# The lead-in of a state-space kernel: norm powers, taps from PSUM, moments, a row of b, W_D as a diagonal

## The chip, the cores and the metric

The kernel runs on one core of one Trainium2 chip. The metric is device time in microseconds (us) of one launch; the kernel before takes 1954.29 us, the median of three runs (1954.05 to 1954.67). Five engines work side by side, each on its own in-order queue, and wait for each other on semaphores: PE (TensorE, matrix products), DVE (VectorE), ACT (ScalarE), POOL (GpSimd) and SP (SyncE, which here only issues DMA transfers). SBUF is the working memory and PSUM holds the results of PE.

## The reference, cut to what matters

Input x is 4 sequences of 1024 rows of 256 numbers. Four layers follow each other: a selective state-space layer, a layer with routed experts and an MLP, a linear attention, and the second layer's kind once more. The change touches the first layer alone:

```python
rn = resid * rsqrt(mean(resid * resid, -1) + EPS) * norm_w   # resid = layernorm(x)
skip, x_in = rn @ skip_w.T, rn @ in_w.T
xp = pad(x_in, (K - 1, 0))
conv = conv_b + sum(xp[:, k:k + L, :] * conv_w[:, k] for k in range(K))   # K = 4 taps
x = silu(conv)
delta = softplus(x @ wd1.T @ wd2.T + wd2_b)
Bm, Cm = x @ wB.T, x @ wC.T
h = exp(delta * A) * h + (delta * x) * b          # a scan over the rows, N = 16 states
y = sum_n h * c + x * W_D
return resid + (y * silu(skip)) @ out_w.T
```

So each row is normalised twice: by a layernorm, then by its root mean square.

## The kernel before, in words

The 4096 rows are cut into 8 groups of G = 512; E = 512 channels make EC = 4 tiles of 128 partitions ("channels" 0 to 3 below). `ssm` runs the first layer with an order written out by hand: `Pinned` keeps every instruction in program order on its engine. The main loop (from L941) goes over `s` = group x state and two halves: DVE does two scans (`tensor_tensor_scan`, L966) and two weighted sums (`sum_up`, L918) per half; ACT makes the decays `a` (`decay`, L907), POOL the inputs `u` = dx x row of b (`times_b`, L888), PE transposes h. The rows of b come from DRAM: `row` (L880) has SP broadcast one row to 128 partitions into a tile `bt`, of which there are two. Beside the scan of one group, `prepare` readies the next, and `tick` chooses what else is put between.

The first group has nothing to hide beside, so `first_group` (L715) is its own piece, the lead-in, and it ends with the first scan:

- SP loads the x of group 0 in four pieces, in_wT, skip_wT and the x of group 1 (L184 to L190); ACT's queue issues the small weights and then out_wT and down_w (L191 to L201).
- PE transposes the identity 48 times into a bank that nobody reads (L720).
- `moments(0)` gives mean and variance on DVE. The two norms' factors s1 and s2 are made one after the other (L727 to L733): a power on POOL, three small DVE operations, a second power on POOL, one more DVE operation. Then DVE normalises (`rn`, L739), PE transposes, DVE and ACT take one half each to SBUF with norm_w (`rnT`).
- `w_in(c)` (L760) multiplies by in_wT, one PSUM bank per channel. `taken` (L767) has ACT copy the bank to `xin` in SBUF, behind three columns of zeros, and apply the last tap and conv_b into `xc`; DVE adds the other three taps from `xin`, shifted.
- Per channel, ACT's silu, then PE's products with wd1 (`dt1`) and wbcT (`bc`). `taken(2)` and `taken(3)` stand between the silus. After them come the moments and factors of group 1 (L793 to L797) and b1, s1 of group 0.
- DVE copies `dt1` and `bc` out; `bc` goes to DRAM; PE multiplies by wd2 (`z`), ACT makes `delta` (Softplus), DVE `dx`. The first row of b is a product with ones (`b0`, in PSUM), which DVE copies to a `bt` tile (L821).
- W_D x xc is made in place, channels 0 and 1 on POOL (L837), 2 and 3 on ACT (L860); PE transposes the result into `acc` in the steps q = 1 and q = 2 (L863).

SP's next loads are the second row of b (L933), the x of groups 2 and 3, and small router weights.

Of the kernel before, what the change touches and what calls it, by code (L numbers as in the profile page):

```python
# [12 lines left out]
F32 = mybir.dt.float32  # L13
AF = mybir.ActivationFunctionType
ALU = mybir.AluOpType
# [35 lines left out]
class Net:  # L51
# [89 lines left out]
    def ssm(self, xs, hs, behind):  # L141
# [6 lines left out]
        with ExitStack() as ctx:  # L148
# [39 lines left out]
            skip_w0 = spare[:, :KD, :]  # L188
            sp.dma_start(out=skip_w0, in_=io["skip_wT"].rearrange("(k p) m -> p k m", p=P))
            load_x(1)  # L190
# [9 lines left out]
            out_w = self.load_rows(late, "out_wT", EC, D)  # L200
            down_w = self.load_rows(late, "down_w", IC, D)  # L201
# [4 lines left out]
            def rsqrt(out, v):  # L206
                pool.tensor_scalar(out, v, EPS, None, ALU.add)
                pool.tensor_tensor(out, out, self.mhalf.to_broadcast(list(out.shape)), ALU.pow)
# [47 lines left out]
            def factors(g, less, var):  # L256
                s1 = late4.tile([P, TG], F32, tag="s1", name="s1")
                s2 = late4.tile([P, TG], F32, tag="s2", name="s2")
                rsqrt(s1, var)
                yield 0  # L260
                pool.tensor_tensor(s2, s1, s1, ALU.mult)
                pool.tensor_tensor(s2, s2, var, ALU.mult)
                rsqrt(s2, s2)
                yield 0
                pool.tensor_tensor(s2, s2, s1, ALU.mult)
# [13 lines left out]
            def bank(shape, name):  # L279
                return mm.tile(shape, F32, tag="mm", name=name)  # L280
# [434 lines left out]
            def first_group():  # L715
# [4 lines left out]
                for i in range(48):  # L720
                    pe.transpose(cold[:, :P], self.ident, self.ident)
                mhalf = self.mhalf.to_broadcast([P, TG])
# [3 lines left out]
                b1, b2 = (late2.tile([P, TG], F32, tag=f"{n}0", name=n) for n in ("b1", "b2"))  # L726
                dve.tensor_scalar(s1, var, EPS, None, ALU.add)  # L727
                pool.tensor_tensor(s1, s1, mhalf, ALU.pow)
                dve.tensor_tensor(s2, s1, s1, ALU.mult)
                dve.tensor_tensor(s2, s2, var, ALU.mult)  # L730
                dve.tensor_scalar(s2, s2, EPS, None, ALU.add)
                pool.tensor_tensor(s2, s2, mhalf, ALU.pow)
                dve.tensor_tensor(s2, s2, s1, ALU.mult)  # L733
# [16 lines left out]
                xin = one.tile([P, EC, KC - 1 + G], F32, tag="xe", name="xin")  # L750
                pool.memset(xin[:, :, : KC - 1], 0.0)
# [40 lines left out]
                act.copy(carry, xin[:, :, G:])  # L792
                mv = moments(1)  # L793
                less = late2.tile([P, TG], F32, tag="sum", name="less1")
                pool.tensor_scalar(less, mv[:, :, 0], -1.0, None, ALU.mult)
                for _ in factors(1, less, mv[:, :, 1]):
                    pass  # L797
                pool.tensor_tensor(b1, mean, s1, ALU.mult)
                pool.tensor_scalar(b1, b1, -1.0, None, ALU.mult)
                pool.tensor_scalar(s1, s1, 1.0, None, ALU.add)  # L800
# [9 lines left out]
                bts[0] = thr.tile([P, G], F32, tag="bt", name="bt")  # L810
                for c in range(EC):
                    ps = bank([P, G], "z")
                    mul(ps, [(wd2[:, c * P : (c + 1) * P], dt1)])
                    act.activation(delta[:, c, :], ps, AF.Softplus, bias=wd2_b[:, c : c + 1])
                    if c == 1:

                        b0 = hp.tile([P, G], F32, tag="hT", name="b0")
                        mul(b0, [(ones, bc[:1, :])])
                for c in range(EC):
                    if c == 2:  # L820
                        dve.tensor_copy(bts[0], b0)  # L821
                    dve.tensor_tensor(dx[:, c, :], delta[:, c, :], xc[:, c, :], ALU.mult)
# [31 lines left out]
                def start(q):  # L854

                    decay(2 * q + 2)
                    decay(2 * q + 3)
                    if q == 0:
                        evac(cT, ps[:, :, N:])
                        for c in (2, 3):  # L860
                            evac(xc[:, c, :], xc[:, c, :], scale=w_d_col[:, c : c + 1])
                        return
                    pair = [(t, begun(xc, t)) for t in (2 * q - 2, 2 * q - 1)]  # L863
                    for t, p in pair:
                        evac(acc[:, t, :], p)
# [67 lines left out]
            row(1)  # L933
            for g in range(2, 4):
                load_x(g)
# [894 lines left out]
```

## Time and profile before

| | us |
|---|---|
| median of 3 runs | 1954.29 |
| the profiled execution | 1952.51 |
| its span, first to last instruction | 1950.8 |
| DVE, PE, ACT, POOL busy | 1545.6, 1772.8, 1178.8, 924.2 |
| first `rn` / first tap / `dt1` copy / first scan start | 9.39 / 15.39 / 27.20 / 35.63 |
| fifth scan / ninth scan start | 42.21 / 49.88 |

The profile comes from one execution. A line of its timeline has the start in us from the span's start, the duration (of several merged instructions, xcount, from the first start to the last end), the engine, the source line, the operation with out<-in, and in brackets how long the engine had been idle and what released it. Nearly every line says L46, that of the helper that pins the order, so instructions are told apart by their tiles. "skip_w" is also the name shown for views into the same buffer (`spare`), such as `rnT`. A matmul of 32-bit numbers shows as two records. A line of the table by windows gives the bounds, then the length, then the busy time of PE, PEld (its weight loads), DVE, ACT and POOL, then PEclk, the clock granted to TensorE as a share of full speed.

The lead-in is the first 36 us of 1951. From there to about 1100 us DVE paces the layer: its busy time is 98.23 of the 100 us from 100 to 200, and 386.39 of the 400 us from 400 to 800.

### The profile page before, as it was taken

What the parts mean: (1) busy time and instruction counts of PE and PEld (TensorE: products, weight loads), DVE (VectorE), ACT (ScalarE), POOL (GpSimd) and SP (SyncE); (2) the same over time, 40 slices, a digit from 0 to 9 for tenths busy, and PEclk for the clock granted to TensorE, in tenths of its full rate; (3) what the DMA queues carried; (4) which work ended last, traced back from release to release, by engine and by line L of the source; (5) the groups of instructions that cost most, each with busy time, mean ns of one, the idle gap of its engine ahead of it and who ended that gap; (6) DMA issues with size and microseconds to landing.
All of it is one profiled execution on the core that took longest, in us unless ns stands there. A gap on an engine that the chain in (4) does not pass through costs nothing.

```text
span 1950.8 us, 22751 instructions
## 1 busy us (share of the span) xinstructions
PE 1772.8 (91%) x7450; PEld 1141.0 (58%) x7450; DVE 1545.6 (79%) x2637; ACT 1178.8 (60%) x2335; POOL 924.2 (47%) x746
## 2 busy tenths in 40 slices
PE   7777789989899898898878999899999999999999
PEld 4445446556456564564645756666666566655665
DVE  6999999999999999999999989834549655434551
ACT  5877788887987878877564663844434333323330
POOL 4978998899888998888861000121111000000000
PEclk9969799999999999999989999999999999999999
DMA  4111121221212212212123121110000000000000
GB/s 142 49 39 55 50 81 55 82 72 64 88 57 80 69 51 87 77 45 80 55 89 122 60 81 49 60 65 1 1 1 1 11 11 12 0 12 11 11 11 11
DMA packets 79927, 97.47 MB, mean 50 GB/s; under 512 B 7360, under 2 KB 53312, under 8 KB 79808
## 3 DMA queue, kind: packets, MB, share of 16 engines
q1 hardware_dynamic: 74592, 90.66, 14.9%
q10 hardware_dynamic: 5216, 5.36, 0.9%
q8 instruction: 59, 0.97, 0.2%
q14 instruction: 60, 0.49, 0.1%
HBM read 83.15 MB, written 12.85 MB: 49 GB/s over the span
## 4 chain that ended last, share of the span: by engine, by line
PE 34%; DVE 13%; ACT 5%; issue 1%; POOL 1%; DVEq 0%; ACTq 0%; POOLq 0%
PE ps L135 23%; PE o L46 2%; PE at L46 1%; PE up L46 1%; DVE eq L46 1%; DVE acc L46 1%; DVE eq L1397 1%; DVE code L1405 1%; PE st L1469 1%; DVE h L46 1%; DVE tb L46 1%; PE route L1303 1%; PE down L46 1%; ACT tb L46 1%; PE emb L46 1%
## 5 line engine op out<-in xcount | busy, mean ns | idle before, releaser
L46 POOL TENSOR_TENSOR u<-dx,bt 128x1024 f32<-128x1024 f32 x255 | 601.6, 2361 | 79.7 <-DVE h L46 69.7
L46 DVE TENSOR_TENSOR_SCAN h<-a,u 128x512 f32<-128x512 f32 x512 | 608.2, 1226 | 16.8 <-ACT a L46 14.4
L46 PE MATMUL hT<-ident,h 128*128 128x128 f32 x2048 | 310.5, 292 | 105.4 <-DVE acc L46 105.1
L46 ACT ACTIVATE a<-delta,a_neg 128x512 f32<-128x512 f32 x512 | 340.1, 689 | 96.5 <-DVE h L46 95.7
L46 PEld LDWEIGHTS hT<-ident,h 128*128 128x128 f32 x2048 | 245.4, 149 | 242.8 <-DVE acc L46 196.6
L46 DVE SCALAR_TENSOR_TENSOR acc<-hT,cT,acc 128x512 f32<-128x512 f32 x512 | 354.2, 731 | 13.5 <-PE hT L46 12.8
L1726 DVE TENSOR_TENSOR act<-s,ps 128x512 f32<-128x512 f32 x64 | 43.9, 686 | 146.3 <-PE ps L135 145.5
L46 PE MATMUL up<-hT,up_w 128*128 128x512 f32 x256 | 134.6, 652 | 10.1 <-ACT up_v L46 10.0
L1724 ACT ACTIVATE s<-ps 128x512 f32<-128x512 f32 x64 | 38.2, 597 | 162.7 <-PE ps L135 162.6
L46 PE MATMUL gate<-hT,gate_w 128*128 128x512 f32 x256 | 122.1, 600 | 0.0
L135 PE MATMUL ps<-hT,w_gate_w 128*128 128x512 f32 x256 | 120.6, 592 | 0.0
L135 PE MATMUL ps<-hT,w_up_w 128*128 128x512 f32 x256 | 120.5, 592 | 0.0
L135 PE MATMUL ps<-w_down_w,act 128*128 128x256 f32 x512 | 117.5, 381 | 3.0 <-DVE x L1500 3.0
L46 PE MATMUL down<-w_down_w,av 128*128 128x256 f32 x512 | 118.2, 379 | 0.0
L46 POOL TENSOR_TENSOR xc<-xc,tap 128x512 f32<-128x512 f32 x84 | 108.8, 1296 | 18.8 <-ACT tap L46 18.7
L135 PEld LDWEIGHTS ps<-w_down_w,act 128*128 128x128 f32 x512 | 95.7, 190 | 21.4 <-DVE x L1500 8.8
L46 ACT ACT_TABLE_LOAD x77 | 98.8, 1283 | 14.8 <-DMA w_wd2T<-in_wd2T 7.3
L46 PEld LDWEIGHTS down<-w_down_w,av 128*128 128x128 f32 x512 | 94.8, 190 | 17.0 <-issue 5.3
L1387 ACT ACTIVATE tb<-d,ex 128x64 f32<-128x64 f32 x256 | 62.0, 333 | 53.9 <-DVE ex L1377 53.9
L46 PEld LDWEIGHTS up<-hT,up_w 128*128 128x128 f32 x256 | 48.8, 206 | 60.6 <-issue 42.0
L46 PE MATMUL out<-w_out_wT,y 128*128 128x256 f32 x256 | 67.6, 411 | 18.3 <-DVE y L46 18.3
L135 PEld LDWEIGHTS ps<-hT,w_up_w 128*128 128x128 f32 x256 | 48.5, 190 | 57.7 <-issue 56.4
(299 smaller groups left out, 3032.4 us busy)
## 6 DMA issues: line engine op xcount, KB each, us to landing
bt<-bcd SPq DMA_DIRECT2D x127, 256.0 KB, 3.3
gate_w<-in_gate_w SPq DMA_DIRECT2D x64, 128.0 KB, 2.3
up_w<-in_up_w SPq DMA_DIRECT2D x64, 128.0 KB, 2.2
in_wT<-in_in_wT SPq DMA_DIRECT2D x8, 512.0 KB, 5.0
hs<-hT SPq DMA_DIRECT2D x8, 512.0 KB, 2.9
xs<-xw SPq DMA_DIRECT2D x8, 512.0 KB, 2.7
hT<-hs SPq DMA_DIRECT2D x8, 512.0 KB, 4.9
x<-xs SPq DMA_DIRECT2D x8, 512.0 KB, 4.2
```

The costliest lines, as they stand in the source:

```text
L46: return self.tc.keep_in_program_order(f(*args, **kw))
L135: self.nc.tensor.matmul(ps, lhsT=lhsT, rhs=rhs, start=i == 0, stop=i == len(pairs) - 1)
L1303: nc.tensor.matmul(ps[:, t, m, :], lhsT=h[:, k, col], rhs=w["scores"][t][:, k, :], start=k == 0, stop=k == KD - 1,)
L1387: nc.scalar.activation(tbv[:, m, i, :], d[:, M4 + m, 0:NKEY], AF.Copy, scale=ex[:, m, i : i + 1],)
L1397: dve.tensor_tensor(eq, v[:, M4:, :].unsqueeze(2).to_broadcast(shk), r[:, M4:, :].unsqueeze(3).to_broadcast(shk), ALU.is_gt,)
L1405: dve.tensor_reduce(code.rearrange("p m j -> p (m j)"), eq.rearrange("p m j b -> p (m j) b"), AX.X, ALU.add,)
L1469: self.nc.tensor.transpose(st[:, c, :], tb[:, i, c * P : (c + 1) * P], self.ident)
L1724: nc.scalar.activation(s, pg, AF.Silu)
L1726: nc.vector.tensor_tensor(a, s, pu, ALU.mult)
```

## The change

1. The two powers no longer follow each other: with var the variance, s2 = ((1+EPS) var + EPS²)^-½ is taken directly, and s1 = (var + EPS)^-½ beside it. In the first group the order is s2, then s1; in `factors` (all later groups) three small POOL operations fall away.
2. The taps read the PSUM bank instead of `xin`; the ACT copy to `xin` goes, and a copy of three columns to `carry`, once per channel, is put behind the taps. The first tap of channel 3 goes to ACT and POOL.
3. `taken(2)` and `taken(3)` both stand behind the first silu. The moments and factors of group 1 move up, ahead of the taps; on SP the x of group 1 moves ahead of skip_wT.
4. The first row of b comes through DRAM, like the others (`row(0)`); `b0` stays for the first two `u`. The product b0 moves behind the four z.
5. W_D x xc is a PE product with a diagonal matrix that POOL makes from the identity; it writes `acc`'s start in the steps q = 0 and q = 1.
6. out_wT and down_w are loaded by SP, behind the second row of b and ahead of the x of groups 2 and 3.
7. 40 idle transposes instead of 48.

```diff
@@ ssm: loads, factors
+            load_x(1)
             sp.dma_start(out=skip_w0, in_=io["skip_wT"].rearrange("(k p) m -> p k m", p=P))
-            load_x(1)
...
-            out_w = self.load_rows(late, "out_wT", EC, D)
-            down_w = self.load_rows(late, "down_w", IC, D)
...
+            def both_norms(eng, out, var):
+                eng.tensor_scalar(out, var, 1.0 + EPS, EPS * EPS, ALU.mult, ALU.add)
@@ first_group
-                for i in range(48):
+                for i in range(40):
                     pe.transpose(cold[:, :P], self.ident, self.ident)
...
+                both_norms(dve, s2, var)
+                rsqrt(s2)
                 dve.tensor_scalar(s1, var, EPS, None, ALU.add)
-                pool.tensor_tensor(s1, s1, mhalf, ALU.pow)
-                dve.tensor_tensor(s2, s1, s1, ALU.mult)
-                dve.tensor_tensor(s2, s2, var, ALU.mult)
-                dve.tensor_scalar(s2, s2, EPS, None, ALU.add)
-                pool.tensor_tensor(s2, s2, mhalf, ALU.pow)
-                dve.tensor_tensor(s2, s2, s1, ALU.mult)
+                rsqrt(s1)
...
+                w_d = spare[:, 2 * KD, :].rearrange("p (c e) -> p c e", c=EC)
+                for c in range(EC):
+                    pool.tensor_scalar(
+                        w_d[:, c, :], self.ident, w_d_col[:, c : c + 1], None, ALU.mult
+                    )
+                mv = moments(1)
...
                 def taken(c, ps):
-                    act.copy(xin[:, c, KC - 1 :], ps)
                     act.activation(
                         xc[:, c, :], ps, AF.Identity, scale=conv_w[:, c, KC - 1 :],
                         bias=conv_b[:, c : c + 1],
                     )
                     for k in range(KC - 1):
-                        dve.scalar_tensor_tensor(
-                            xc[:, c, :], xin[:, c, k : k + G], conv_w[:, c, k : k + 1],
-                            xc[:, c, :], ALU.mult, ALU.add,
-                        )
+                        late = KC - 1 - k
+                        to, part, by = xc[:, c, late:], ps[:, : G - late], conv_w[:, c, k : k + 1]
+                        if c == EC - 1 and k == 0:
+                            t = spare[:, 2 * KD + 1, : G - late]
+                            act.activation(t, part, AF.Copy, scale=by)
+                            pool.tensor_tensor(to, to, t, ALU.add)
+                        else:
+                            dve.scalar_tensor_tensor(to, part, by, to, ALU.mult, ALU.add)
+                    act.copy(carry[:, c, :], ps[:, G - KC + 1 :])
...
                     act.activation(xc[:, c, :], xc[:, c, :], AF.Silu)
-                    if c + 2 < EC:
-                        taken(c + 2, xins[c + 2])
                     if c == 0:
+                        taken(2, xins[2])
+                        taken(3, xins[3])
                         sums = bank([P, G], "dt1"), bank([2 * N, G], "bc")
...
-                bts[0] = thr.tile([P, G], F32, tag="bt", name="bt")
+                row(0)
...
-                for c in (0, 1):
-                    pool.tensor_scalar(
-                        xc[:, c, :], xc[:, c, :], w_d_col[:, c : c + 1], None, ALU.mult
-                    )
+                def by_w_d(t):
+                    ps = bank([P, E], "xdT")
+                    for c in range(EC):
+                        pe.matmul(
+                            ps[:, c * P : (c + 1) * P], lhsT=xc[:, c, t * P : (t + 1) * P],
+                            rhs=w_d[:, c, :], start=True, stop=True,
+                        )
+                    return ps
@@ after first_group
             row(1)
+            out_w = self.load_rows(late, "out_wT", EC, D, sp)
+            down_w = self.load_rows(late, "down_w", IC, D, sp)
```

More of the change, by code (lines that the diff above doesn't have):

```diff
@@ L204, in ssm, with rsqrt @@
             carry = wp.tile([P, EC, KC - 1], F32, tag="carry", name="carry")
-            def rsqrt(out, v):
-                pool.tensor_scalar(out, v, EPS, None, ALU.add)
-                pool.tensor_tensor(out, out, self.mhalf.to_broadcast(list(out.shape)), ALU.pow)
+            def rsqrt(v):
+                pool.tensor_tensor(v, v, self.mhalf.to_broadcast(list(v.shape)), ALU.pow)
+            def both_norms(eng, out, var):
+                eng.tensor_scalar(out, var, 1.0 + EPS, EPS * EPS, ALU.mult, ALU.add)
             def moments(g):
@@ L258, in factors @@
                 s2 = late4.tile([P, TG], F32, tag="s2", name="s2")
-                rsqrt(s1, var)
+                both_norms(pool, s2, var)
+                rsqrt(s2)
                 yield 0
-                pool.tensor_tensor(s2, s1, s1, ALU.mult)
-                pool.tensor_tensor(s2, s2, var, ALU.mult)
-                rsqrt(s2, s2)
+                pool.tensor_scalar(s1, var, EPS, None, ALU.add)
+                rsqrt(s1)
                 yield 0
-                pool.tensor_tensor(s2, s2, s1, ALU.mult)
                 b1, b2 = shift(s1, less, f"b1{g % 2}"), shift(s2, less, f"b2{g % 2}")
@@ L719, in first_group @@
                 cold = hp.tile([P, E], F32, tag="hT", name="cold")
-                for i in range(48):
+                for i in range(40):
                     pe.transpose(cold[:, :P], self.ident, self.ident)
-                mhalf = self.mhalf.to_broadcast([P, TG])
                 mv = moments(0)
@@ L726, in first_group @@
                 b1, b2 = (late2.tile([P, TG], F32, tag=f"{n}0", name=n) for n in ("b1", "b2"))
+                both_norms(dve, s2, var)
+                rsqrt(s2)
                 dve.tensor_scalar(s1, var, EPS, None, ALU.add)
-                pool.tensor_tensor(s1, s1, mhalf, ALU.pow)
-                dve.tensor_tensor(s2, s1, s1, ALU.mult)
-                dve.tensor_tensor(s2, s2, var, ALU.mult)
-                dve.tensor_scalar(s2, s2, EPS, None, ALU.add)
-                pool.tensor_tensor(s2, s2, mhalf, ALU.pow)
-                dve.tensor_tensor(s2, s2, s1, ALU.mult)
+                rsqrt(s1)
                 dve.scalar_tensor_tensor(b2, mean, -1.0, s2, ALU.mult, ALU.mult)
@@ L749, in first_group @@
                 act.activation(a_neg, a_neg, AF.Copy, scale=-1.0)
-                xin = one.tile([P, EC, KC - 1 + G], F32, tag="xe", name="xin")
-                pool.memset(xin[:, :, : KC - 1], 0.0)
+                pool.tensor_tensor(b1, mean, s1, ALU.mult)
+                pool.tensor_scalar(b1, b1, -1.0, None, ALU.mult)
+                pool.tensor_scalar(s1, s1, 1.0, None, ALU.add)
+                w_d = spare[:, 2 * KD, :].rearrange("p (c e) -> p c e", c=EC)
[4 more added lines that the diff above has]
+                mv = moments(1)
+                less = late2.tile([P, TG], F32, tag="sum", name="less1")
+                pool.tensor_scalar(less, mv[:, :, 0], -1.0, None, ALU.mult)
+                for _ in factors(1, less, mv[:, :, 1]):
+                    pass
                 xc = one.tile([P, EC, G], F32, tag="xc", name="xc")
@@ L791, in first_group @@
                     mul(sums[1], [(wbc[:, c, :], xc[:, c, :])], *at)
[L792 to L800, printed above, removed]
                 dt1 = one.tile([P, G], F32, tag="db", name="dt1")
@@ L814, in first_group @@
                     act.activation(delta[:, c, :], ps, AF.Softplus, bias=wd2_b[:, c : c + 1])
-                    if c == 1:
-                        b0 = hp.tile([P, G], F32, tag="hT", name="b0")
-                        mul(b0, [(ones, bc[:1, :])])
+                b0 = hp.tile([P, G], F32, tag="hT", name="b0")
+                mul(b0, [(ones, bc[:1, :])])
                 for c in range(EC):
-                    if c == 2:
-                        dve.tensor_copy(bts[0], b0)
                     dve.tensor_tensor(dx[:, c, :], delta[:, c, :], xc[:, c, :], ALU.mult)
@@ L859, in start @@
                         evac(cT, ps[:, :, N:])
[L860 to L865, printed above, removed]
+                    if q < 2:
+                        for t, p in [(t, by_w_d(t)) for t in (2 * q, 2 * q + 1)]:
+                            evac(acc[:, t, :], p)
                 starts.append(start)
```

## The prediction

> **What bounds the kernel now.** I read the table by windows first, then the timeline of the first 60 us engine by engine, then the waits. The chain of waits on the page reaches back only to about 850 us and says nothing here. Between 34 and 900 us DVE waits 11.4 us for ACT's `a`, 10.9 for PE's hT, 5.0 for PE's `down` and 2.0, once, for POOL's `u`: it paces the layer, so a lead-in that ends x us later should end the kernel about x later. The lead-in is a chain from engine to engine:
>
> ```profile
> 5.99 0.17 DVE L46 TENSOR_SCALAR s<-mv 128x4 f32<-128x4 f32 x1
> 6.25 1.02 POOL L46 TENSOR_TENSOR s<-s,mhalf 128x4 f32<-128x4 f32 x1 [3.81 <-DVE s L46]
> 7.95 1.01 POOL L46 TENSOR_TENSOR s<-s,mhalf 128x4 f32<-128x4 f32 x1 [0.68 <-DVE s L46]
> 9.39 1.38 DVE L46 TENSOR_SCALAR rn<-xw,s,b 128x256 f32<-128x256 f32 x4
> ...
> 14.02 0.58 ACT L46 COPY xin<-xin 128x512 f32<-128x512 f32 x1 [1.60 <-PE xin L46]
> 14.50 0.78 ACT L46 ACTIVATE xc<-xin,w_conv_b,w_conv_w 128x512 f32<-128x512 f32 x1
> 15.39 4.57 DVE L46 SCALAR_TENSOR_TENSOR xc<-xin,w_conv_w,xc 128x512 f32<-128x512 f32 x6 [3.44 <-ACT xc L46]
> 17.02 1.28 ACT L46 ACT_TABLE_LOAD   x1
> 20.13 4.56 DVE L46 SCALAR_TENSOR_TENSOR xc<-xin,w_conv_w,xc 128x512 f32<-128x512 f32 x6 [0.18 <-ACT xc L46]
> 25.41 1.12 PE L46 MATMUL dt<-xc,w_wd1T 128*128 128x512 f32 x2
> 27.20 0.66 DVE L46 COPY dt<-dt 128x512 f32<-128x512 f32 x1
> 35.63 4.57 DVE L46 TENSOR_TENSOR_SCAN h<-a,u 128x512 f32<-128x512 f32 x4
> 36.73 3.12 POOL L46 TENSOR_SCALAR xc<-xc,w_W_D 128x512 f32<-128x512 f32 x2
> 42.21 2.34 DVE L46 TENSOR_TENSOR_SCAN h<-a,u 128x512 f32<-128x512 f32 x2 [2.02 <-POOL u L46]
> 49.88 2.34 DVE L46 TENSOR_TENSOR_SCAN h<-a,u 128x512 f32<-128x512 f32 x2 [0.48 <-ACT a L46]
> ```
>
> The reader should see two powers in a row; twelve taps on DVE without a hole over 0.18 us, because ACT runs ahead of DVE; and the fifth scan waiting 2.02 us for a `u` that stood behind POOL's W_D products.
>
> **1. Norm.** With one power, b2 can start at 7.31, where the first small operation starts now (7.31), and `rn` 0.20 later, at 7.51 instead of 9.39: **-1.88**. PE's 40 transposes end near 8.1 (48 end at 9.27; weight loads 0.145 apart), beside the first `rn`: nothing. A_log and W_D land at 10.6 and 10.8 (issued 4.68 and 5.93, 5.9 and 4.9 to landing); the first is used by 11.5, the second by POOL alone.
>
> **2. First tap.** Without the copy to `xin` (14.02 to 14.50) ACT's `xc` starts at 14.02 - 1.88 = 12.14, and the first tap at 12.14 + 0.78 + 0.11 = **13.03** instead of 15.39. Group 1's moments (2.6, 24.61 to 27.20) now stand before it on DVE, from 10.1 to 12.7, if x has landed. It takes skip_wT's place in SP's queue, which was issued at 3.55 and landed after 6.5, at 10.05: just in time. POOL's diagonal (four 128x128 products, each between 0.23 for 128x4 and 1.57 for 128x512; 0.55 by width) and the factors run from 10.8 to about 17, to 20 at worst; POOL is needed at 25.6.
>
> **3. The taps: here the change loses.** In the built program's list of instructions with their waits, ACT's three-column copy to `carry` waits for VectorE's count 29, and 29 is reached by the third tap of channel 0; likewise 32, 35 and 37 for the others. ACT's next `xc` stands behind that copy, so ACT no longer runs ahead: per channel, `xc` 0.78, to DVE 0.11, three taps, to ACT 0.05, copy 0.10 until the next starts. A tap that reads PSUM is not in the trace: between 0.66 (copy from PSUM) and 0.76 (the taps' step now); `acc`, with an operand in PSUM, shows 0.731, the taps 0.751. I take 0.76; eleven at 0.66 would give 1.1 back. So taps start at 13.03 (c0) and 13.03 + 3.33 = 16.36 (c1), ending at 18.64; copy 0.24, table load 1.28 (no longer beside taps), silu 0.53 until `xc`, 0.89: c2 at 21.58 to 23.86; `xc` of c3 at 24.0, the part tap on ACT 24.67 to 25.41, POOL's addition 25.55 to 26.83 (1.28, from `xc<-xc,tap`), two taps to 28.40, copy, and only then silu of c1, 28.55 to 29.18. PE must still do five products before `dt1` is complete (dt and bc of c1 and c2, dt of c3), each two records of 0.43, the step of `xin`'s 16 records in 7.13: 4.3, and 0.15 to DVE. `dt1` copy at **33.7** instead of 27.20: **+6.5**.
>
> The Trainium skill's page "PSUM — Partial Sum Buffer", section "PSUM bank collisions raise a hardware error", says that two engines must not touch one bank at once, reads against reads included; no run here shows a collision. By it the wait is no accident of the scheduler: the change's readers must take turns, which speaks against tapping the bank from two engines. By the rule the sum stands at 1960.2; with free readers it would be the third rival's 1947.7.
>
> **4. PE's clock.** PE then idles from 17.25 (end of `xin`) to 29.2 but for two products near 21 to 23. The table by windows shows what that does:
>
> ```profile
> 30.17:33.59 3.42, 3.05 (x10) 1.00 (x8) 2.30 (x4) 1.83 (x3) 2.51 (x8) 1.00 0.44 106
> 33.59:37.00 3.41, 0.00 (x0) 0.00 (x0) 3.26 (x5) 3.31 (x5) 2.60 (x2) 1.00 1.02 334
> 37.00:40.41 3.41, 0.97 (x4) 0.68 (x5) 3.19 (x3) 3.13 (x6) 3.41 (x3) 0.50 0.36 86
> 40.41:43.83 3.42, 3.42 (x18) 3.42 (x18) 1.62 (x2) 2.71 (x6) 3.42 (x2) 0.50 0.01 2
> 43.83:47.24 3.41, 3.12 (x23) 2.44 (x22) 3.41 (x5) 3.41 (x8) 3.41 (x3) 1.00 0.32 83
> ```
>
> After a window of 3.41 us in which PE did nothing, the next has half the clock, until one is full of work. Any last whole window before 29.2 holds at most 0.5 us of PE work, so the five products should begin at half speed (skip's records are 0.85 apart at 0.50, 0.43 at 1.00). The clock returns at a window's end, 2.5 to 6 us later: about 4.3 us cost half their work, **+2.2** (bounds: 0, if the clock holds; +4.3, all ten records).
>
> **5. From `dt1` to the first scan.** Now 8.43. The b0 product between z 1 and z 2 and DVE's copy of it go: z of channel 3 gives `delta` at +4.45 to 5.14, table load to 6.43, `a`; DVE's dx and u end at 7.15; first scan at +7.2: **-1.2**.
>
> **6. First to ninth scan.** Now 14.25, with 2.02 and 0.48 of waiting. POOL no longer multiplies by W_D (3.12) and ACT not either (1.33), so the 2.02 goes. Two things come up instead. Row 0 lands as late as 3.25 + 4.4 = 7.65 after the `dt1` copy (bcd issued at +1.65, 1.6 to landing, then row 1's time of today; 3.1, later rows' time, is the other end): u, 2.35, holds the third scan 0.55 (0 to 0.6). ACT does all four acc copies before the `a` of the second half: about 0.4 (0 to 1). Net **-1.55** (-2.5 to -0.9). The diagonal products are not in the trace: 32 records of 0.145 (transposes' loads) to 0.43 (512 columns), 4.6 to 13.8; I take 0.19, the usual weight load, 6.1 us on PE between z and hT, where PE idles 5.14 today; beyond that up to 7 could fall on hT's way, though DVE's other work covers about 1.
>
> **7. The rest.** 1.5 MB more stand in SP's queue ahead of row 2; ACT's queue gets shorter, beside a wait for rn. out_wT and down_w are not used before group 0 ends. In the later groups POOL saves three operations of 0.2 each, beside a DVE that waited for POOL once: 0.
>
> **Sum:** 6.5 + 2.2 - 1.2 - 1.55 = **+5.95**. Span 1950.8 + 5.95 = 1956.75; with the 1.71 around it (1952.51 - 1950.8) 1958.5. The profiled execution stood 1.78 below the median, so the median comes to **1960.2**.
>
> **Rivals.**
> *The clock holds* (15%): PE idle, but not by a whole window: +3.75, 1958.0. Against it: the table above, and 91.6 to 105.3 at 0.50 behind a window with 1.18 us of work.
> *Row 2 is late* (16%). In the built program SP issues it only when down_w's semaphore is complete. With 1 MB taking 10.1 today, issued at +4.6, that is +14.7, row 2 lands +18.1, its u is ready at +20.5 against a need at +19.9; behind the x of groups 2 and 3 (1 MB, about 3 at 350 GB/s) it is 0.6 to 3.6 more: 1961 to 1964. For me: out of ACT's queue it shared with 2 MB then, and I expect +12.
> *Faster* (6%): ACT is not held. If its copies passed the taps, eleven taps would follow each other from 13.03 to 21.4, silu to 22.1, dt to 23.3: `dt1` at 23.4, -3.8 - 1.2 - 1.55: 1947.7. It decides itself at the second channel: if DVE waits under 0.3 us between c0 and c1, this is it. ACT is an in-order queue in every row of the trace, and the list of waits is plain.
> *No difference* (5%): the scans take the delay up: 1954. Against it: 98.23 us of 100 busy.
>
> My own forecast has 58%: 1958.3 to 1962.5. What a measurement of this kernel can tell from no change is about 0.2%, 3.9 us: slower means over 1958.2. Nearly all of my forecast lies there (55 of 58), 40% of the first rival (6) and all of the second (16): slower 0.77; the rest of these two and the fourth: same 0.17; faster 0.06. The range leaves out the third and fourth and the late half of the second's tail: 1956 to 1963.5; its lower end takes the clock's holding with quicker taps (1958.0 - 1.1), its upper the clock's upper bound or a late row.
>
> **What would show it.** The taps in groups of three with about 1.05 us of DVE idle between c0 and c1, released by ACT `xc`; `rn` at 7.5 and first tap at 13.0; `dt1` copy at 34 to 37; half the clock near 30 us; scans without POOL's 2.02. Wrong it would be if x of group 1 lands after 10.1, if the taps run on, or if row 2's load holds POOL.

## The result, and the profile after

The changed kernel takes 1963.93 us (median of five, 1958.45 to 1965.55) against 1954.29: the ratio is 1.0046, 95% interval 1.003 to 1.0062. Measured again on another occasion it took 1964.96 (six, 1958.77 to 1966.82) against 1953.13: 1.0055, 1.0042 to 1.0068. It is slower, as forecast. The forecast's 1960.2 is 3.7 us short, and 1963.93 lies 0.4 above its range. The profiled execution took 1965.55, with a span of 1963.5: 12.7 more than before.

The timeline of that execution, to be held against the lines of before (same columns; start first, then duration):

```profile
7.78 1.38 DVE L46 TENSOR_SCALAR rn<-xw,s,b 128x256 f32<-128x256 f32 x4
...
11.25 0.43 DVE L46 BATCH_NORM_STATS2 st<-xw 128x6 f32<-128x256 f32 x1 [0.91 <-DMA xw<-in_x]
...
13.06 0.26 ACT L46 ACTIVATE a_neg<-w_A_log 128x64 f32<-128x64 f32 x1 [2.67 <-DMA w_A_log<-in_A_log]
...
14.30 2.32 DVE L46 SCALAR_TENSOR_TENSOR xc<-xin,w_conv_w,xc 128x509 f32<-128x509 f32 x3 [0.37 <-ACT xc L46]
16.65 0.16 ACT L46 COPY carry<-xin 128x3 f32<-128x3 f32 x1 [2.38 <-DVE xc L46]
...
17.53 2.32 DVE L46 SCALAR_TENSOR_TENSOR xc<-xin,w_conv_w,xc 128x509 f32<-128x509 f32 x3 [0.91 <-ACT xc L46]
...
27.65 1.53 DVE L46 SCALAR_TENSOR_TENSOR xc<-xin,w_conv_w,xc 128x510 f32<-128x510 f32 x2 [2.65 <-POOL xc L46]
...
29.96 2.08 PE L46 MATMUL dt<-xc,w_wd1T 128*128 128x512 f32 x2 [4.29 <-ACT xc L46]
...
38.03 0.69 DVE L46 COPY dt<-dt 128x512 f32<-128x512 f32 x1 [8.85 <-PE dt L46]
...
45.36 2.34 DVE L46 TENSOR_TENSOR_SCAN h<-a,u 128x512 f32<-128x512 f32 x2
...
49.08 4.64 DVE L46 TENSOR_TENSOR_SCAN h<-a,u 128x512 f32<-128x512 f32 x4 [1.38 <-POOL u L46]
...
59.51 2.34 DVE L46 TENSOR_TENSOR_SCAN h<-a,u 128x512 f32<-128x512 f32 x2 [0.94 <-POOL u L46]
```

Read down it: `rn` is earlier (7.78 for 9.39). The taps come in threes with holes between, where they ran through before. ACT's three-column copy waits 2.38 us for the third tap, and only then can ACT's next `xc` start, and DVE's next taps wait for that. The `dt1` copy is at 38.03 for 27.20, the first scan at 45.36 for 35.63. The W_D wait (2.02) is gone; a wait for row 0 (1.38) and a longer one at the ninth scan (0.94 for 0.48) have come.

The table by windows of the same execution, around the products (window, length, PE, PEld, DVE, ACT and POOL busy, granted clock):

```profile
25.80:29.21 3.41, 0.00 (x0) 0.00 (x0) 1.50 (x2) 0.65 (x2) 1.08 (x1) 1.00 0.00 0
29.21:32.62 3.41, 2.66 (x3) 0.69 (x4) 0.00 (x0) 3.01 (x5) 0.00 (x0) 0.50 0.00 0
32.62:36.03 3.41, 3.41 (x5) 0.68 (x4) 0.00 (x0) 0.00 (x0) 0.00 (x0) 0.50 0.00 0
36.03:39.45 3.42, 3.42 (x8) 0.75 (x7) 1.14 (x2) 0.00 (x0) 0.00 (x0) 1.00 0.00 0
```

An empty window, then two at half the clock, which hold the first three of the five products and the start of the fourth.

The lead-in is not the whole of it. The starts of some scans in three executions (no. counts from 0, so no. 8 is the prediction's ninth); "again" is the profiled execution of the second occasion:

| | no. 0 | no. 8 | no. 32 | end of span |
|---|---|---|---|---|
| before | 35.6 | 49.9 | 94.7 | 1950.8 |
| after | 45.4 | 59.5 | 107.7 | 1963.5 |
| after, again | 43.0 | 55.8 | 104.0 | 1959.9 |
| after less before | +9.7 | +9.6 | +13.0 | +12.7 |
| again less before | +7.3 | +5.9 | +9.3 | +9.1 |

In both, about 3.4 us are lost between no. 8 and no. 32, where the prediction had put nothing. The timeline of the first of the two there, DVE and POOL:

```profile
80.59 2.36 POOL L46 TENSOR_TENSOR u<-dx,bt 128x1024 f32<-128x1024 f32 x1
80.79 7.98 DVE L46 TENSOR_TENSOR_SCAN h<-a,u 128x512 f32<-128x512 f32 x2
82.90 1.27 POOL L46 TENSOR_TENSOR xc<-xc,tap 128x512 f32<-128x512 f32 x1
84.13 2.34 POOL L46 TENSOR_TENSOR u<-dx,bt 128x1024 f32<-128x1024 f32 x1
86.43 1.26 POOL L46 TENSOR_TENSOR xc<-xc,tap 128x512 f32<-128x512 f32 x1
...
88.85 2.36 POOL L46 TENSOR_TENSOR u<-dx,bt 128x1024 f32<-128x1024 f32 x1 [1.16 <-DVE h L46]
```

The same place before:

```profile
71.91 3.85 DVE L46 TENSOR_TENSOR_SCAN h<-a,u 128x512 f32<-128x512 f32 x2
72.31 2.37 POOL L46 TENSOR_TENSOR u<-dx,bt 128x1024 f32<-128x1024 f32 x1
...
75.02 1.80 POOL L46 TENSOR_TENSOR xc<-xc,tap 128x512 f32<-128x512 f32 x1 [0.34 <-ACT tap L46]
```

Two scans take 7.98 us where two take 2.34. The first is 1.21; the second, no. 21, starts at 81.92 and takes 6.85. It ends 1.1 us after POOL has its first hole, at 87.69. That hole is a wait for this very scan: POOL's next `u`, at 88.85, is released by DVE's h, 0.08 behind the scan's end, since it goes into the buffer (one of four) of the `u` that scans no. 20 and 21 read. No wait of DVE names this: the scan has started, so DVE counts as busy. In the built program, 28 of the 512 scans take their decay from SBUF (L995, `decay(2 * q + 3, True)`, made ahead of an ACT table load) and the others from PSUM. Of the scans from PSUM none takes over 1.23 us; the 28 lose 12.0 us together before and 13.3 after. No. 21 is one of the 28. It takes 2.72 before, where POOL waited 0.34 for ACT's tap in time.

### The profile page after: what moved, and what is told of

It is laid out like the page before. It is cut to its first block, busy times and chain, and to the rows that moved or that the text cites. A ratio compares the mean times of both kernels' runs of the same rounds, so it can differ in the third digit from the quotient of the medians.

```text
span 1963.5 us, 22734 instructions
## 1 busy us (share of the span) xinstructions
PE 1778.2 (91%) x7458; PEld 1144.1 (58%) x7458; DVE 1545.6 (79%) x2632; ACT 1176.6 (60%) x2333; POOL 919.6 (47%) x727
## 3 DMA queue, kind: packets, MB, share of 16 engines
HBM read 83.41 MB, written 12.85 MB: 49 GB/s over the span
## 4 chain that ended last, share of the span: by engine, by line
PE 34%; DVE 13%; ACT 4%; issue 1%; POOL 1%; DVEq 0%; ACTq 0%; POOLq 0%
PE ps L135 22%; PE o L46 2%; PE at L46 1%; DVE acc L46 1%; DVE eq L46 1%; PE up L46 1%; DVE eq L1400 1%; DVE code L1408 1%; DVE h L46 1%; PE down L46 1%; PE st L1472 1%; PE emb L46 1%; DVE tb L46 1%; PE route L1306 1%; PE tr L126 1%
## 5 line engine op out<-in xcount | busy, mean ns | idle before, releaser
L46 DVE SCALAR_TENSOR_TENSOR acc<-hT,cT,acc 128x512 f32<-128x512 f32 x512 | 354.2, 731 | 12.4 <-PE hT L46 11.8
```

The costliest lines, as they stand in the source:

```text
L46: return self.tc.keep_in_program_order(f(*args, **kw))
```

## The experiments

The theory: ACT is held by the ordering of its carry copies behind DVE's taps on one PSUM tile; that and the half clock make the lead-in later; and the later loss is a scan with both operands in SBUF, kept out by POOL. The rivals: the PSUM source itself is slow; the late row 2 or row 0 is the main loss; the long scan only shows a delay from elsewhere. Times differ a little between occasions, so ratios to the kernel before, run beside each, are compared.

| | us | ratio, 95% interval | `dt1` copy | no. 0 | no. 0 to no. 8 | no. 21 takes |
|---|---|---|---|---|---|---|
| before | 1954.29 | 1 | 27.20 | 35.63 | 14.25 | 2.72 |
| after | 1963.93 | 1.0046 [1.003, 1.0062] | 38.03 | 45.36 | 14.15 | 6.85 |
| after, again | 1964.96 | 1.0055 [1.0042, 1.0068] | 35.65 | 42.98 | 12.83 | 6.71 |
| carry on DVE | 1952.65 | 0.9988 [0.998, 0.9997] | 26.20 | 33.53 | 14.22 | 6.23 |
| PE kept busy | 1961.32 | 1.0033 [1.0021, 1.0045] | 34.40 | 41.73 | 12.55 | 6.42 |
| loads on ACT | 1960.55 | 1.0027 [1.0016, 1.0037] | 38.21 | 45.54 | 13.51 | 3.07 |
| taps from a copy | 1952.36 | 0.9989 [0.998, 0.9997] | 27.34 | 34.67 | 14.83 | 6.25 |
| one `a` in PSUM | 1958.15 | 1.0034 [1.0021, 1.0048] | 36.34 | 43.67 | 14.51 | 1.2 |
| carry on DVE, loads later | 1949.60 | 0.9986 [0.9972, 1.0] | 25.29 | 32.63 | 13.59 | 3.27 |
| and row 0 by copy | 1948.96 | 0.9985 [0.9972, 0.9998] | 25.12 | 33.18 | 11.87 | 2.94 |
| loads later, all `a` in PSUM | 1970.90 | 1.0098 [1.0081, 1.0115] | 25.40 | 32.73 | 11.88 | under 1.25 |
| row 0 by copy, one `a` in PSUM | 1944.46 | 0.9962 [0.995, 0.9973] | 25.20 | 33.26 | 11.84 | 1.2 |

### Carry copies on DVE

```diff
-                    act.copy(carry[:, c, :], ps[:, G - KC + 1 :])
+                    dve.tensor_copy(carry[:, c, :], ps[:, G - KC + 1 :])
```

> The changed kernel with one edit: the copy of three columns to `carry` is made by VectorE instead of ScalarE, so ScalarE no longer has a copy between two channels that waits for VectorE's taps. Theory (ScalarE is held by that copy, and PE idles into half clock because of it): the taps run nearly without holes, the `dt1` copy moves from 38.0 us to about 25.3, the five products show 0.43 us a record, the first scan starts near 32.6 (before: 35.6), and the time falls from 1964 to about 1951 (1948 to 1955). Rival (the loss comes from the moved moments, which wait for x of group 1, or from taps that are slow out of PSUM): the time stays within 3 us of 1964.

Its timeline:

```profile
14.17 2.32 DVE L46 SCALAR_TENSOR_TENSOR xc<-xin,w_conv_w,xc 128x509 f32<-128x509 f32 x3 [0.29 <-ACT xc L46]
14.55 0.78 ACT L46 ACTIVATE xc<-xin,w_conv_b,w_conv_w 128x512 f32<-128x512 f32 x1 [0.41 <-PE xin L46]
...
16.40 0.15 DVE L46 COPY carry<-xin 128x3 f32<-128x3 f32 x1
16.47 2.31 DVE L46 SCALAR_TENSOR_TENSOR xc<-xin,w_conv_w,xc 128x509 f32<-128x509 f32 x3
...
19.19 2.31 DVE L46 SCALAR_TENSOR_TENSOR xc<-xin,w_conv_w,xc 128x509 f32<-128x509 f32 x3 [0.34 <-ACT xc L46]
...
26.20 0.69 DVE L46 COPY dt<-dt 128x512 f32<-128x512 f32 x1 [3.00 <-PE dt L46]
```

ACT's second `xc` (14.55, from the second channel's PSUM tile) now runs beside the first channel's taps; the hole between c0 and c1 is gone, and so are 11.3 us of the time. Taps read PSUM here too, three in 2.31: their source costs next to nothing (0.77 a tap, 0.76 from SBUF). What cost was a copy of three columns, 0.16 us long, in the wrong queue. The products run at full clock (granted 1.00 from 19.70 to 26.50), with no hole of PE over 0.6 us ahead of them. The `dt1` copy and the first scan came 0.9 later than expected (26.20 for 25.3, 33.53 for 32.6): the first tap stood at 14.17, with A_log not used before 12.93.

### PE kept busy

26 and 36 idle transposes in PE's holes:

```diff
+                for i in range(26):
+                    pe.transpose(cold[:, :P], self.ident, self.ident)
...
+                    if c == 0:
+                        for i in range(36):
+                            pe.transpose(cold[:, :P], self.ident, self.ident)
```

> The changed kernel with 26 more idle transposes on PE behind the products `xin` and 36 behind the products of channel 0, which fill PE's two holes; nothing else. Theory (the half clock costs the five last products 3.6 us of the 8.07 that lie between the first of them and the `dt1` copy): these products show 0.43 us a record, the `dt1` copy comes 3 to 3.6 us earlier, near 34.5, and the time falls to about 1960. Rival (the clock is a side effect, something else holds `dt1`): the copy stays near 38 and the time near 1964.

Its timeline, first product and the copy behind the five:

```profile
29.17 1.12 PE L46 MATMUL dt<-xc,w_wd1T 128*128 128x512 f32 x2 [1.75 <-ACT xc L46]
...
34.40 0.69 DVE L46 COPY dt<-dt 128x512 f32<-128x512 f32 x1 [6.00 <-PE dt L46]
```

The five products take 5.23 us, and 8.07 in the changed kernel (29.96 to 38.03): the half clock costs 2.84 in that execution. In the other one (28.68 to 35.65, 6.97) it costs 1.74, since the clock came back sooner behind the first product. The median falls by 2.6, but the intervals of the two ratios overlap; what the clock costs is read from the timeline.

### out_wT and down_w on ACT's queue, as before

```diff
-            out_w = self.load_rows(late, "out_wT", EC, D, sp)
-            down_w = self.load_rows(late, "down_w", IC, D, sp)
...
+            out_w = self.load_rows(late, "out_wT", EC, D)
+            down_w = self.load_rows(late, "down_w", IC, D)
```

> The changed kernel with the loads of out_wT and down_w back on ScalarE's queue, ahead of everything, as in the kernel before. Theory (row 2 of b is late because its load waits for down_w's semaphore, and it costs 0.94 us at the ninth scan, and POOL, which then runs behind without a hole, keeps one later scan from starting): POOL's wait of 3.44 us for `bt` goes, the ninth scan starts 14.25 - 1.4 us after the first or less, the time is 1959 to 1963. Against it, the loads share the DMA engines with x of group 1 again, so that the first tap may come up to 1 us later. Rival (the late row is hidden): the time stays at 1964.

POOL's timeline, where the changed kernel has `u` in two pieces with 3.44 us between, waiting for row 2:

```profile
47.11 16.25 POOL L46 TENSOR_TENSOR u<-dx,bt 128x1024 f32<-128x1024 f32 x7 [18.29 <-DMA bt<-bcd]
```

Row 2 is in time (issued 6.1 us behind row 0), so the second rival of the prediction did happen in the changed kernel: there SP issued row 2 at 52.82, 10 us behind row 0, and its `u` came 0.94 late for the ninth scan. The ninth scan is 13.51 behind the first, not the 12.85 or less that was expected, because the third scan waits 1.61 for row 0. The more important number is in the table: no. 21 takes 3.07. With rows in time POOL is ahead of ACT's taps: its addition ahead of this scan waited 0.52 for a tap, and the next got its tap at 84.05, just as POOL's `u` ended at 84.20. There the scan went in, with no hole to be seen in POOL's records, and the addition took 2.16 instead of 1.27. In the changed kernel, with row 2 late, the tap for that addition was ready at 83.88 and POOL came to it at 86.43; there the scan was passed over. The first tap stood at 15.51 here, 1.2 later: the fourth piece of x came later (`rn` at 8.37), and the first four records of `xin` ran at half the clock, 0.85 apart instead of 0.43, after a stretch in which PE had little to do (busy 1.44 of the 3.40 us from 7.40 on; the 40 transposes end at 7.4). A part of the gain is hidden by that. In time it is not clear of the changed kernel's first measurement (the intervals overlap), only of the second.

### Taps from a copy in SBUF

Part 2 undone alone: `xin`, its copy on ACT, twelve taps from it, and the old order of `taken`.

> The changed kernel with part 2 undone alone: ScalarE copies each bank to `xin`, the taps read that, all twelve on VectorE, `taken(2)` and `taken(3)` between the silus, one copy to `carry` at the end. The other parts stay. Theory (only part 2 loses; the rest gains 1.9 at the norm, 1.1 behind the `dt1` copy, and the moments no longer stand between the taps and the `dt1` copy): first tap near 14.9, `dt1` copy near 26.1 (before 27.2), first scan near 33.4, time about 1952 (1949 to 1956). Rival (another part loses, too): over 1956.

Its timeline:

```profile
16.05 4.56 DVE L46 SCALAR_TENSOR_TENSOR xc<-xin,w_conv_w,xc 128x512 f32<-128x512 f32 x6 [2.26 <-ACT xc L46]
20.90 4.56 DVE L46 SCALAR_TENSOR_TENSOR xc<-xin,w_conv_w,xc 128x512 f32<-128x512 f32 x6 [0.28 <-ACT xc L46]
27.34 0.69 DVE L46 COPY dt<-dt 128x512 f32<-128x512 f32 x1 [1.88 <-PE dt L46]
```

The time expected came out; first tap, `dt1` copy and first scan were each 1.2 later than expected (16.05, 27.34, 34.67). Part 2 by itself is thus the whole slowdown and more: without it the other parts together gain 0.0011 of the time (interval 0.0003 to 0.002), about 2 us. And of part 2, by the first experiment (0.9988 with that line alone moved), it is the one line of the carry copy.

### One decay in PSUM

```diff
-   lambda: (decay(2 * q + 2), decay(2 * q + 3, True), decay(2 * q + 4))
+   lambda: (decay(2 * q + 2), decay(2 * q + 3, q != 9), decay(2 * q + 4))
```

> The changed kernel; only the decay of scan no. 21 goes to PSUM instead of SBUF. Theory (this scan is starved by POOL because it reads two operands from SBUF): it takes 1.2 us instead of 6.85, nothing else waits for it, and the kernel loses 4.1 (what it lost against the kernel before) to 5.6 us: 1959.3 (1958 to 1961). Rival (the long record only shows a delay that comes from elsewhere, POOL's u or ACT's a being late): DVE waits about 5 us there instead, and the time stays at 1963.9.

Its timeline; the first line holds no. 20 and no. 21:

```profile
80.03 2.33 DVE L46 TENSOR_TENSOR_SCAN h<-a,u 128x512 f32<-128x512 f32 x2
...
86.16 1.22 DVE L46 TENSOR_TENSOR_SCAN h<-a,u 128x512 f32<-128x512 f32 x1 [1.37 <-ACT a L46]
```

The two take 2.33 instead of 7.98, beside the same POOL operations. So the scan lost its time to its SBUF operand, and nothing else was late behind it. A part comes back: ACT, which had to wait for one more scan, is 1.37 late two scans on. Net, no. 8 to no. 32 takes 44.6 us instead of 48.2, and 44.8 before. All twelve profiles of the kernel agree: 48.2 to 48.3 in the five where no. 21 takes over 6 us, 44.6 to 46.0 in the seven others. The ratio falls by 0.0012 to 0.0021, 2 to 4 us, but the intervals overlap: the timeline carries this, not the time.

### Carry on DVE and the two loads later

As the first experiment, with out_wT and down_w issued by SP in the main loop:

```diff
+                if s == 2:
+                    out_w = self.load_rows(late, "out_wT", EC, D, sp)
+                    down_w = self.load_rows(late, "down_w", IC, D, sp)
```

> Carry copies on DVE as in the first experiment (1952.65), and out_wT and down_w issued by SP only at the third state's step, behind rows 2 and 3 of b. Theory (the late row costs the ninth scan 0.9 us, and by pushing POOL's work together it starves scan no. 21 for another 3 to 4): ninth scan at 14.3 less 0.9 after the first or better, scan 21 at about 3 us; 1948.5 (1947 to 1950). Rival (scan 21 is starved by the earlier lead-in itself, not by the late row): 1951.8.

No. 21 takes 3.27 instead of 6.23, and no. 0 to no. 32 takes 59.6 instead of 62.5: the theory's mechanism. The time does not show it: the ratio is 0.9986, the first experiment's 0.9988, while the expected 1948.5 is 0.997 of the 1954.3 that it was reckoned from, and the rival's 1951.8 is 0.9987. What no. 21 gives back is seen in this stretch alone. The third scan still waits 1.68 for row 0.

### Row 0 by a copy

```diff
-                row(0)
+                bts[0] = thr.tile([P, G], F32, tag="bt", name="bt")
...
                 for c in range(EC):
+                    if c == 3:
+                        dve.tensor_copy(bts[0], b0)
```

> As the kernel with later loads, and row 0 of b not through DRAM: DVE copies the product b0 to the bt tile ahead of the fourth dx. Theory (the third scan waits 1.5 us for row 0's u; the copy costs at most 0.66 ahead of the first scan): third scan without a wait, 1947.4 (1946.3 to 1948.5). Rival (the copy stands on the way to the first scan for its whole 0.66 and the third scan's wait was covered later): 1948.5 to 1949.5.

Its timeline:

```profile
30.77 0.69 DVE L46 COPY bt<-b 128x512 f32<-128x512 f32 x1 [0.50 <-PE b L46]
...
33.18 6.79 DVE L46 TENSOR_TENSOR_SCAN h<-a,u 128x512 f32<-128x512 f32 x6
```

The first scan is 8.06 behind the `dt1` copy, 0.7 more than with part 4; but six scans now run without a wait. No. 0 to no. 8 falls by 1.7 against the run above. Part 4 alone therefore gains 0.7 ahead of the scan and loses up to 1.7 behind it. That loss comes and goes: the third scan waited 1.4 to 1.7 in six profiles with row 0 through DRAM, and not at all in three. In the six SP issued row 0 only 3.2 to 3.5 us behind the store of bc that it waits for, in the three 1.6 behind. In time the net gain is too small to be seen.

### All decays in PSUM

`decay(2 * q + 3)` without the spare tile, for all 28, on the kernel with later loads.

> As the kernel with later loads, and the 28 decays that went to SBUF go to PSUM, so that ACT must wait for one scan more before each. Theory (scans whose decay is in SBUF lose 7 to 12 us to POOL in all, also in the kernel before): no scan over 1.25 us, 1941.5 (1939 to 1945). Rival (the SBUF copies are there because ACT would be late: DVE waits for ACT's a as much as it gains): 1948.5.

The rival holds, and more than that: 21 us slower than the kernel it is made from. No scan is over 1.25 us any more and the 512 scans take 6.8 us less (618.6 for 625.4). But DVE waits longer for ACT's `a` (32.5 us between 30 and 1030, 18.9 in the kernel it is made from) and for hT (16.5, 11.3). The last scan starts 16.6 later; these waits, with 1.7 less for POOL's `u`, less the scans' gain account for some 10 of it; the rest is open. So the SBUF copies gain more than they lose, and PSUM was the better place only where a scan was starved for long.

### A scan against POOL by itself

> Not the computation: zeros go to the output, and nine stretches measure three DVE operations of 128x512 that start just behind n POOL products of 128x1024 (2.35 us each). Scans with a and u in SBUF: n = 0, 1, 2, 4, 8. With n = 4: scans with a in PSUM, products with two operands in SBUF, products with one in PSUM, one-operand products. Theory (a POOL operation that is under way or follows without a hole keeps DVE from its second SBUF operand): 1.2 us per scan with n = 0; the first scan ends only with POOL's last product, after about 2.4, 4.7, 9.4 and 18.8 us; 1.2 with a in PSUM. Rival (both engines share the port at a lower rate): every scan is slower by the same factor while POOL runs, about 2.3, whatever n.

The timeline; three DVE operations a line, with n = 0, 1 and 8 POOL products for the first three lines, and n = 4 for the others:

```profile
4.02 3.45 DVE L46 TENSOR_TENSOR_SCAN hsb<-a_sb,u 128x512 f32<-128x512 f32 x3
...
8.47 5.50 DVE L46 TENSOR_TENSOR_SCAN hsb<-a_sb,u 128x512 f32<-128x512 f32 x3
...
36.15 9.70 DVE L46 TENSOR_TENSOR_SCAN hsb<-a_sb,u 128x512 f32<-128x512 f32 x3
...
57.86 3.44 DVE L46 TENSOR_TENSOR_SCAN hps<-a_ps,u 128x512 f32<-128x512 f32 x3
...
67.62 8.22 DVE L46 TENSOR_TENSOR htt<-a_sb,u 128x512 f32<-128x512 f32 x3
...
78.74 1.88 DVE L46 TENSOR_TENSOR hpt<-a_ps,u 128x512 f32<-128x512 f32 x3
...
88.52 7.43 DVE L46 TENSOR_SCALAR hts<-u 128x512 f32<-128x512 f32 x3
```

Neither theory nor rival is right as a whole. With n = 8 the scans do not wait for the row's end: each takes 3.27 to 3.29 and the two engines take turns, one operation each (POOL's products go from a step of 2.30 to 3.2). So a scan waits for the POOL operation under way, about 2.1 us, and then goes in. What holds of the theory: with `a` in PSUM POOL is not felt at all; two SBUF operands wait, and so does a one-operand DVE operation from SBUF to SBUF.

### Which row of operations holds

> Not the computation: zeros go to the output, and eight stretches each put one scan with a and u in SBUF beside a row of POOL operations without a hole: products of 128x1024 (u), additions of 128x512 in place (as xc<-xc,tap), or the two in turn; the scan is asked for at once, or behind one or two scans with a in PSUM. The run before showed a scan that gets in at the first boundary between two u. Theory (the alternation with additions keeps POOL ahead, as in the kernel, where three boundaries were passed): with u alone 3.3 us or less, with u and additions in turn the scan ends only with the row, 10 us or more. Rival (the kind of operation does not matter, what counts is when the scan asks): all stretches asked for at once show 3.3 or less, all asked for late over 5.

Two lines of its timeline, u and additions in turn, asked for at once and behind one scan:

```profile
30.05 3.27 DVE L46 TENSOR_TENSOR_SCAN hua_at<-a_sb,u 128x512 f32<-128x512 f32 x1
...
46.74 2.14 DVE L46 TENSOR_TENSOR_SCAN hua_at<-a_sb,u 128x512 f32<-128x512 f32 x1
```

No stretch shows over 3.34. Both expectations fall: neither the kind of operation nor the moment of asking makes POOL pass a boundary here. In the kernel it passed three, in each of the five profiles with 6.2 to 6.9 us, and each time the scan came in where POOL's next `u` had to wait for it (1.16 us). With the loads on ACT, and with carry on DVE and loads later, the same scan went in at a boundary without a hole. Why one boundary lets it in and another does not is open.

### The changed kernel again, and the best version

> The changed kernel itself once more, beside the next one on the same chip. Both theories: 1963.9 (1958 to 1966), ratio 1.0046 to the kernel before.

> The changed kernel with carry copies on DVE, out_wT and down_w issued at the third state's step, row 0 by DVE's copy, and the decay of scan no. 21 in PSUM. Theory: as without the last edit (1948.96) less the 1.7 that this scan still lost there: ratio to the kernel before 0.9975 (0.996 to 0.9985). Rival (ACT, which then waits for one scan more, gives it back): 0.9985.

The second has four edits on the changed kernel, all shown above: carry copies on DVE, later loads, row 0 by copy, `q != 9`. It takes 1944.46 (1943.55 to 1949.63) beside 1953.13 for the kernel before and 1964.96 for the changed one: faster than the kernel before by 0.27 to 0.5%, and 20.5 us faster than the changed one. The expected 0.9975 (0.996 to 0.9985) holds it; how the gain over 0.9985 divides between this edit and chance the intervals do not settle.

The changed kernel's second profile is the best check of the prediction, because there the loads of the lead-in came much as it had assumed (A_log used at 11.63, 13.06 in the first):

```profile
13.02 2.32 DVE L46 SCALAR_TENSOR_TENSOR xc<-xin,w_conv_w,xc 128x509 f32<-128x509 f32 x3 [0.28 <-ACT xc L46]
...
35.65 0.69 DVE L46 COPY dt<-dt 128x512 f32<-128x512 f32 x1 [7.75 <-PE dt L46]
...
42.98 6.80 DVE L46 TENSOR_TENSOR_SCAN h<-a,u 128x512 f32<-128x512 f32 x6
...
55.81 1.22 DVE L46 TENSOR_TENSOR_SCAN h<-a,u 128x512 f32<-128x512 f32 x1 [1.19 <-POOL u L46]
```

First tap 13.02 (13.03 was forecast), `dt1` copy 35.65 (33.7 + 2.2 = 35.9), no. 8 later than before by 5.93 (5.95).

## Why the prediction was right, and where it fell short

- **1, Norm.** Forecast -1.88, found -1.61 and -1.81; the fourth piece of x landed 0.27 later in the first execution.
- **2, First tap.** Forecast 13.03, found 14.30 and 13.02. "Just in time" was too thin. Two loads that the first tap depends on came late in the first profile: x of group 1 was waited for (moments from 11.25), and A_log, issued on ACT's queue ahead of the first `xc`, was not "used by 11.5" but at 13.06. The first was named as what would make the forecast wrong; the second was not, and it sets the time: DVE was through with the moments at 13.93 and then waited 0.37 for ACT's `xc`. Together they are worth 1.3 us.
- **3, The taps.** The mechanism is as forecast and shown by the first experiment. The taps' part took 15.66 us from the first tap to the first product, 16.2 forecast. Mis-sized is the term of the products: five were put at 4.3 us from `xin`'s step, and take 5.1 at full clock (dt and bc in turn start 1.0 apart, not 0.86). The trace of before had this: its last dt starts at 25.41 and the bc behind it at 26.47. The price of a tap from PSUM, 0.76, was right. The page "PSUM — Partial Sum Buffer" had its readers take turns (section "PSUM bank collisions raise a hardware error"). What the runs show is narrower: ordering waits of the built program, which go when both instructions stand in one queue; no run shows a collision.
- **4, PE's clock.** Forecast +2.2, found +2.84 and +1.74. The bounds held. "Until one is full of work" was too strict: the clock also came back behind windows with 3.20 us of work (101.85 to 105.27 before) and 3.28 (22.39 to 25.80 after). The windows' edges lie elsewhere in each execution (30.17 and 33.59 before, 25.80 and 29.21 after), so idle time alone does not set the cost: 4.29 us of it ahead of the five products cost 2.84, 5.18 us only 1.74. The page "TensorE: Matmul & The Clock Gate", section "Part 1: The HAM clock gate (the "warmup" mystery)", says that the window runs free of the kernel's start; these edges agree.
- **5, From `dt1` to the first scan.** Forecast 7.2, found 7.33 in both.
- **6, First to ninth scan.** Forecast 12.70, found 14.15 and 12.83. The 2.02 of W_D went as forecast. Row 0's wait was put at 0.55; it was 1.38 and nothing, as its issue came 3.2 and 1.6 us behind that of the store of bc (1.6 was assumed). ACT's four copies, put at 0.4, show in no wait of DVE, and the diagonal products, put at 6.1 us of PE, took 4.1. Row 2 was late by 0.94 and 1.19: the rival with 16% happened in its small form. Its terms were right (the issue 14.8 and 13.3 behind the `dt1` copy, 14.7 by its sum, and 0.6 and more of waiting); that its 1961 to 1964 also holds the result is owed more to the next step.
- **7, The rest: 0.** This is the step that failed: +3.4 between no. 8 and no. 32 in both. The 1.5 MB more in SP's queue, put at nothing here, bring it on: with these loads on ACT or later no. 21 takes 3.07 and 3.27. The sum looked at POOL's waits and at who waits for POOL, and found none. It did not ask what POOL's lack of holes does to DVE operations that read SBUF beside it, though the trace of before has scans of 2.7 us among those of 1.2. The page "SBUF — State Buffer", section "SBUF: two separate sides", has DVE with two SBUF inputs and GpSimd share one pair of ports, locked for a whole instruction. The scan against POOL by itself agrees with that (3.27 us a scan, taking turns); the 6.85 in the kernel is more than one instruction. What ended it is seen, POOL's wait for this scan; why the scan was passed at three boundaries no run here shows.
- **The rivals.** *The clock holds* fell (0.50 in both profiles). *Row 2 is late* came true in part. *Faster* fell at the place it had named: DVE waited 0.91 between c0 and c1, not under 0.3; the first experiment makes it true by other means. *No difference* fell.

With 1.3 (first tap), 0.6 (the clock), 0.8 (the products), 1.45 (to no. 8) and 3.1 (from there to the end), less 0.5 (the taps), the first profile's +12.7 is the forecast's +5.95 and these 6.75. Where the loads come as assumed, 5.9 by the ninth scan and 3.4 from the starved one make 9.3; the medians are later by 9.6 and 11.8. That 5.93 stands so close to 5.95 is partly luck: taps 0.5 and clock 0.5 under the forecast cancel the products' 0.8, and row 2's 1.19, forecast as nothing, stands in for row 0's 0.55 and ACT's 0.4. So the direction and the main mechanism were right by reasoning, and the size fell short by the starved scan.

## What to carry to other kernels

When several engines are moved onto one PSUM tile, list for each queue what each instruction waits for: a 0.16 us copy behind another engine's work can hold its whole queue; in DVE's queue it held the next taps for 0.07 us here (16.40 to 16.47). When a stretch of work is shifted, ask also which engines will afterwards run without holes, and which operations only get on in those holes; here that loss showed as a long duration, not as a wait. Price a load that is "just in time" by its late end as well.

## What the runs showed of the hardware

- A DVE scan of 128x512 with both operands in SBUF takes 1.2 us alone, 3.27 beside POOL products of 2.3 (each engine in turn), and 6.2 to 6.9 at one place in the kernel, in five of twelve profiles, until POOL itself waits for this scan. With the decay in PSUM it takes 1.2 beside any of them. A one-operand SBUF copy with a factor (TENSOR_SCALAR) waits likewise: three take 7.43, and three products with one operand in PSUM 1.88.
- A hole of 0.08 us between two POOL operations is enough in the kernel: scans no. 85, 213 and 341, which take 2.4 to 2.7 us before and after, went in at such a hole. In two profiles scan no. 21 went in without one.
- Taps with a PSUM source cost about the same as from SBUF (0.77 us a step for 128x509 and 0.76 for 128x512).
- With nothing changed in the kernel, the first 6.1 us of the five products ran at half clock in one execution (29.96 to 36.03, behind 4.29 us of idle PE) and the first 3.6 in another (28.68 to 32.3, behind 5.18): 1.1 us apart in the end.
